# Loading early choices' results inside the experts' loop, and splitting the last choices' sums between two engines

## The chip, the cores and the metric

The kernel runs on one core of a Trainium2 chip. The core has five engines that run their own instruction streams: TensorE (PE, matrix products; PEld is its weight loads), VectorE (DVE), ScalarE (ACT), GpSimd (POOL) and SyncE (SP, used here as a queue that issues DMA transfers). An engine executes its stream in order, and waits on semaphores for the others. The metric is the device time of one execution in microseconds. Before the change the median of six runs is 678.52 us (674.44 to 679.24).

## The reference

Four transformer layers follow one another on 1024 tokens of width 256; each is a cross attention and a feed-forward block, both added to x. The change lies in the last block, a mixture of 64 experts of which each token uses 8:

```python
router_logits = x @ gate_w                                  # 1024 x 64
routing_weights, selected = jax.lax.top_k(router_logits, 8)
routing_weights = jax.nn.softmax(routing_weights, axis=-1)
gate = jax.lax.ragged_dot(hidden_sorted, gate_proj_w, group_sizes)
up   = jax.lax.ragged_dot(hidden_sorted, up_proj_w, group_sizes)
down = jax.lax.ragged_dot(jax.nn.silu(gate) * up, down_proj_w, group_sizes)
out  = jnp.sum(down[unsort].reshape(-1, 8, 256) * routing_weights[..., None], axis=1)
```

`hidden_sorted` holds every token's normed row 8 times, sorted by expert; `x` as used here is already normed, and `out` is added to the unnormed x.

## The kernel before

The 1024 tokens are 8 tiles of 128 (`NT = 8`). Everything up to the router is emitted by a planner (`Flow`): threads (`tile3`, `heads3`, `softmax3`, `scatter`, ...) yield operations with an engine and an assumed duration in us (`yield Op(DVE, 1.2, ...)`), and the planner decides from these durations and from due times in which order the operations stand on each engine. A changed duration can thus change the order of later operations.

*Routing* (`tile3`, one thread per tile). VectorE finds the 8 largest logits of each token (`sel`), TensorE counts each token's position within its expert (`pos`), and each chosen expert e gets the slot `e * CAP + pos` with `CAP = 192`. The kernel keeps `v = (NROWS - e * CAP) - pos` for the chosen experts and takes the 8 largest, so a token's choices 0 to 7 are sorted by expert, lowest first. Choice j can therefore only lie in experts up to 56 + j. A token whose position does not fit is marked in `over` (L1573), its rows are sent out of bounds, and it is done in a slow loop over all 64 experts behind a branch (L1757). `scatter` then puts a token's normed row, with the number of its result row, into `hs` in DRAM, with one indirect DMA for each tile and choice, generated by GpSimd (L1637): 64 puts.

*Experts* (`experts`). 32 pairs of experts (`n_pairs = 32`), p = 0 to 31. For each pair SP loads 384 rows (`load_rows`, six pairs ahead, L1739), TensorE turns them (L1800) and multiplies them with gate and up weights (L1849), ScalarE and VectorE make silu times up (L1855, L1857), TensorE multiplies with the down weights (L1867), VectorE and ScalarE copy the results out of PSUM (L1872), and GpSimd puts them with three indirect DMAs into `yd`, at each token's row for that choice (L1874). Weights come in groups of four experts into six buffers of tag `wt`. VectorE also makes one diagonal matrix per pair, of a tile's weights for one choice (L1888); `ON_PE = (4, 5, 6, 7)` names the choices that TensorE adds.

*Results.* `load_results(jp)` loads choices 2jp and 2jp + 1 of all tokens back from `yd` (2 MB) in two halves (jp = 3 in four quarters) on SP's queue, L1815. It waits for the puts of those pairs in which the choices can lie: jp = 0, 1, 2, 3 are issued at pairs 28, 29, 30, 31. The first three take `wt` buffers, the last takes `cx` and `ctxT`.

*Sums* (`sums`). Choices 0 to 3 are added to x by VectorE (`add_result`, L1825, a scalar_tensor_tensor with two inputs in SBUF): four of these 32 adds stand in pair 30, the rest after the loop. Choices 4 to 7 are summed in PSUM by TensorE with the diagonals (`sum_result`, L1830: 32 sums, 64 matmuls), choices 4 and 5 of all tiles first, then 6 and 7 tile by tile. VectorE adds the PSUM tile to x (`add_to_x`, L1708), and ScalarE's queue stores it (L1915). The order in `experts` and `sums` is written out by hand.

Of the kernel before, what the change touches and what calls it, by code (L numbers as in the profile page):

```python
# [25 lines left out]
ALU = mybir.AluOpType  # L26
AX = mybir.AxisListType

P = 128
B, S, D = 4, 256, 256  # L30
NTOK = B * S
NT = NTOK // P
# [14 lines left out]
E3, I3, K3 = 64, 96, 8  # L47
ORDERED = {mybir.EngineType.PE, mybir.EngineType.DVE, mybir.EngineType.Activation,
           mybir.EngineType.Pool}
GROUP, WEIGHTS, FIRST = 4, 6, 2  # L50
AHEAD = 6
ON_PE = (4, 5, 6, 7)
CAP = 192
RPP = 2 * CAP // P
NROWS = E3 * CAP
# [10 lines left out]
PE, DVE, ACT, POOL, SP = "PE", "DVE", "ACT", "POOL", "SP"  # L66
# [160 lines left out]
def model(ctx: ExitStack, tc: tile.TileContext, a: dict, out: bass.AP):  # L227
    nc = tc.nc
    PSUM = bass.MemoryType.PSUM

    const = ctx.enter_context(tc.tile_pool(name="const", bufs=1))
# [11 lines left out]
    def held(pool, shape, name, dtype=F32):  # L243
        return pool.tile(shape, dtype, tag=name, name=name)
# [4 lines left out]
    def x_t(t):  # L249
        return xb[t // 2][:, t % 2, :]  # L250

    ident = held(const, [P, P], "ident")
# [60 lines left out]
        out=tri, in_=tri, pattern=[[1, P]], compare_op=ALU.is_gt, fill=0.0, base=0,  # L313
# [9 lines left out]
    rwo = held(const, [P, NT, E3], "rwo")  # L323
    slots = held(const, [P, NT, K3], "slots", I32)
    over = held(const, [P, NT], "over")
    choice_w = held(const, [P, NT, K3], "choice_w")
    tick = held(const, [1, 1], "tick")

# [65 lines left out]
    def needs(ld, group, wanted, reason):  # L394

        for w in wanted:
            tc.add_manual_dep(
                ld.ins, w.name,
                mybir.DependencyInfo(mybir.DependencyClass.Sync, mybir.DependencyReason.DATA),
                reason=reason,  # L400
            )
        tc.declare_no_dep(ld.ins, group=group, keep=wanted + readers, reason=reason)
        tc.add_to_no_dep_group(group, ld.ins)
        readers.append(ld.ins)

    def layers(nk):
# [1110 lines left out]
        def tile3(t, q, lane, left):  # L1517
# [44 lines left out]
                    ps.ap, onesb if u < t else tri, sel[:, u, :], start=u == 0, stop=u == t  # L1562
                )
            pos, places = ps.ap, Buf()
            yield Op(DVE, 1.2, (ps, SEL[t]), (places,))
            nc.vector.scalar_tensor_tensor(ok, pos, float(CAP), sel[:, t, :], ALU.is_lt, ALU.mult)

            nc.vector.tensor_sub(v, first, pos)
            nc.vector.tensor_mul(v, v, ok)
            nc.vector.max(top[:, 8 : 8 + K3], v)  # L1570

            spilt = over[:, t : t + 1]
            nc.vector.tensor_scalar(spilt, top[:, 7 + K3 : 8 + K3], 0.0, None, ALU.is_equal)  # L1573
            nc.vector.tensor_scalar(rest[:, 0:1], spilt, float(NROWS), float(NROWS), ALU.mult, ALU.add)
            nc.vector.tensor_scalar(
                slots[:, t, :], top[:, 8 : 8 + K3], -1.0, rest[:, 0:1], ALU.mult, ALU.add
# [130 lines left out]
    def add_to_x(t, y):  # L1707
        nc.vector.tensor_add(x_t(t), y, x_t(t))  # L1708
# [3 lines left out]
    def moe_tile(shape, tag, bufs):  # L1712
        return moe.tile(shape, F32, tag=tag, name=tag, bufs=bufs)
# [86 lines left out]
                nc.tensor.transpose(tp[:, j, :], hb[:, j, dc * P : (dc + 1) * P], ident)  # L1800
        return hbT, tps

    def load_results(jp):

        n = 2 if jp == 3 else NT // 2
        for h in range(2):
            if jp < 3:
                g = moe_tile([P, GROUP * (4 * I3 + D)], "wt", WEIGHTS)[:, : NT // 2 * 2 * D]
            else:
                g = (cx.rearrange("p t d -> p (t d)"), ctxT.rearrange("p c r -> p (c r)"))[h]  # L1810
            gats[jp, h] = g = g.rearrange("p (t j d) -> p t j d", t=NT // 2, j=2)
            for t0 in range(0, NT // 2, n):
                at = (h * NT // 2 + t0) * P * K3
                source = yd[at : at + n * P * K3, :].rearrange("(t p j) d -> p t j d", p=P, j=K3)
                ld = nc.sync.dma_start(  # L1815
                    g[:, t0 : t0 + n].rearrange("p t j d -> p t (j d)"),
                    source[:, :, 2 * jp : 2 * jp + 2, :].rearrange("p t j d -> p t (j d)"),
                )
                needs(ld, "back", backs[: RPP * (n_pairs - 3 + jp)], "results of these choices alone")

    def result(t, j):
        return gats[j // 2, t // (NT // 2)][:, t % (NT // 2), j % 2, :]

    def add_result(t, j):
        nc.vector.scalar_tensor_tensor(  # L1825
            x_t(t), result(t, j), choice_w[:, t, j : j + 1], x_t(t), ALU.mult, ALU.add
        )

    def sum_result(y, t, i):
        nc.tensor.matmul(  # L1830
            y, diag[:, t, i, :], result(t, ON_PE[i]), start=i == 0, stop=i == len(ON_PE) - 1
        )

    def experts():
        for p in range(in_early, AHEAD):
            load_rows(p)
        load_weights(FIRST)
        load_weights(FIRST + 1)
        hbT, tps = rows_turned(0)
        nc.scalar.copy(hbT[:, 0], tps[0])  # L1840
        nc.vector.tensor_copy(hbT[:, 1], tps[1])
        for p in range(n_pairs):
            e = 2 * p
            gu, dn = weights[e // GROUP]
            pg, pu = ps_mm([I3, 2, RPP, P // 2], "ps_g3"), ps_mm([I3, 2, RPP, P // 2], "ps_u3")
            for k, ps in enumerate((pg, pu)):
                for i in range(2):
                    for dc in range(2):
                        nc.tensor.matmul(  # L1849
                            ps[:, i], gu[:, (e + i) % GROUP, 2 * k + dc, :],  # L1850
                            hbT[:, dc, :, i * (P // 2) : (i + 1) * (P // 2)],
                            start=dc == 0, stop=dc == 1,
                        )
            g = moe_tile([I3, 2, RPP, P // 2], "g4", 2)
            nc.scalar.activation(g, pg, AF.Silu)  # L1855
            act = moe_tile([I3, 2, RPP, P // 2], "act3", 2)
            nc.vector.tensor_mul(act, pu, g)  # L1857
            if p + 1 < n_pairs:
                hbT, tps = rows_turned(p + 1)
                nc.scalar.copy(hbT[:, 0], tps[0])  # L1860
                nc.vector.tensor_copy(hbT[:, 1], tps[1])
            yb = moe_tile([P, RPP, D], "yb", 3)
            for js in ((0, 1), (2,)):
                y = ps_acc([P, len(js), D], "ps_y")
                for k, j in enumerate(js):
                    for i in range(2):
                        nc.tensor.matmul(  # L1867
                            y[i * (P // 2) : (i + 1) * (P // 2), k], act[:, i, j, :],
                            dn[:, (e + i) % GROUP, :], start=True, stop=True,
                        )  # L1870
                for k, j in enumerate(js):
                    (nc.scalar.copy if j == 1 else nc.vector.tensor_copy)(yb[:, j, :], y[:, k, :])  # L1872
            for j in range(RPP):
                put = nc.gpsimd.indirect_dma_start(  # L1874
                    out=yd[:, :],
                    out_offset=bass.IndirectOffsetOnAxis(
                        ap=hbs[p][:, j, D : D + 1].bitcast(I32), axis=0
                    ),
                    in_=yb[:, j, :], in_offset=None, bounds_check=NPAIR - 1, oob_is_err=False,
                )  # L1880
                tc.declare_no_dep(put.ins, group="back", reason="distinct rows")
                tc.add_to_no_dep_group("back", put.ins)
                backs.append(put.ins)

            n = NT * len(ON_PE)
            for k in range(p * n // n_pairs, (p + 1) * n // n_pairs):
                t, i = k // len(ON_PE), k % len(ON_PE)
                nc.vector.tensor_scalar(  # L1888
                    diag[:, t, i, :], ident, choice_w[:, t, ON_PE[i] : ON_PE[i] + 1], None, ALU.mult
                )  # L1890
            if p + AHEAD < n_pairs:
                load_rows(p + AHEAD)
            k = FIRST + 2 + p if p < WEIGHTS - 2 else p // 2 + WEIGHTS if p % 2 else 0
            if k and k < E3 // GROUP:
                load_weights(k)
            if p >= n_pairs - 4:
                load_results(p - (n_pairs - 4))
            if p == n_pairs - 2:
                for t in range(NT // 2):
                    add_result(t, 0)  # L1900

    def sums():

        ys = [(ps_mm if t < 4 else ps_acc if t < 6 else ps_tp)([P, D], "ps_sum") for t in range(NT)]
        for i in range(len(ON_PE) - 2):
            for t in range(NT):
                sum_result(ys[t], t, i)
        for j in range(K3 - len(ON_PE)):
            for t in range(0 if j else NT // 2, NT):
                add_result(t, j)  # L1910
        for t in range(NT):
            for i in range(len(ON_PE) - 2, len(ON_PE)):
                sum_result(ys[t], t, i)
            add_to_x(t, ys[t])
            nc.scalar.dma_start(out[t // 2, t % 2 * P : (t % 2 + 1) * P, :], x_t(t))  # L1915

    with tc.manual_schedule(engines=ORDERED | {mybir.EngineType.SP}):
        experts()
# [85 lines left out]
```

## Time and profile before

| What | us |
|---|---|
| Median of 6 runs | 678.52 |
| The profiled execution's own time | 677.34 |
| Its span, first to last instruction | 675.6 |
| Routing's last put starts (L1637) | 480.27 |
| First expert matmul (L1849) | 483.54 |
| Period of the experts' loop | 4.99 |
| Last pair's down product starts (L1867) | 644.21 |
| Last add to x starts (L1708) | 671.86 |

| Engine | busy us | share |
|---|---|---|
| PE | 616.5 | 91% |
| DVE | 457.0 | 68% |
| POOL | 403.9 | 60% |
| ACT | 346.7 | 51% |

All times below are counted from the start of the span. The profile's chain follows the work back from the last instruction to whatever released each step. The timeline lists instructions in order of time, merged where they are alike; in brackets is the idle time before an instruction and what ended it. The row of an indirect DMA on POOL is the time that GpSimd takes to generate it; the transfer lands later. The releaser of a wait for several semaphores is the one that came last by the profile.

### The profile page before, as it was taken

How to read it: one execution, taken by the hardware profiler on the slowest of the kernel's cores; microseconds unless marked ns; L12 is line 12 of the kernel's file. 1: busy time of each engine (PE TensorE's matmuls, PEld its weight loads, DVE VectorE, ACT ScalarE, POOL GpSimd, SP SyncE). 2: the span in 40 equal slices, each digit the busy share in tenths (PEclk: the TensorE clock that was granted, in tenths of full speed). 3: DMA queues.
4: the chain of work that ended last, by engine and by line, in shares of the span. 5: the costliest groups of instructions: out<-in, count | busy, mean ns of one | idle time of the engine just before them, and what ended most of it. 6: DMA issues, size and time to landing. Idle time of an engine off the chain costs nothing. (4 is left out here: it accounts for less than half of the span.)

```text
span 675.6 us, 11485 instructions
## 1 busy us (share of the span) xinstructions
PE 616.5 (91%) x3820; PEld 473.7 (70%) x3820; DVE 457.0 (68%) x1161; ACT 346.7 (51%) x894; POOL 403.9 (60%) x516
## 2 busy tenths in 40 slices
PE   5999799999999999999998998995499999999937
PEld 4765465687878766888777786763378788787726
DVE  5787656767898689779789898897143444444482
ACT  1242268468898885457875876874122222222200
POOL 5999897111365484838148778767456555665550
PEclk9999899999999989999999999897599999999979
DMA  8999999710001031000031110222699867874395
GB/s 276 383 386 203 202 207 211 247 48 2 1 12 54 22 107 45 1 1 1 1 103 40 64 63 32 88 72 86 193 320 308 262 216 279 262 222 147 120 338 187
DMA packets 56036, 98.16 MB, mean 145 GB/s; under 512 B 7121, under 2 KB 37576, under 8 KB 55968
## 3 DMA queue, kind: packets, MB, share of 16 engines
q1 hardware_dynamic: 46048, 78.40, 40.4%
q0 software_dynamic: 7680, 16.84, 7.1%
q10 hardware_dynamic: 2240, 2.10, 0.9%
q8 instruction: 33, 0.54, 0.4%
q14 instruction: 35, 0.29, 0.1%
HBM read 58.42 MB, written 43.07 MB: 150 GB/s over the span
## 5 line engine op out<-in xcount | busy, mean ns | idle before, releaser
L1874 POOL DMA_INDIRECT yd<-yb,hb x84 | 85.9, 1023 | 57.7 <-DVE yb L1872 38.5
L1637 POOL DMA_INDIRECT hs<-hx,slots x64 | 66.2, 1034 | 25.7 <-issue 9.7
L1857 DVE TENSOR_TENSOR act<-ps_u,g 96x384 f32<-96x384 f32 x32 | 17.7, 554 | 73.6 <-ACT g L1855 63.6
L852 POOL TENSOR_TENSOR st<-st,mhalf 128x1 f32<-128x1 f32 x56 | 33.3, 598 | 53.4 <-DVE st L848 41.1
L1472 ACT ACTIVATE e<-ps_s,nm 128x128 f32<-128x128 f32 x128 | 46.1, 416 | 15.2 <-DVE nm L1466 15.1
L1439 POOL TENSOR_TENSOR q<-rt 64x512 f32<-64x512 f32 x32 | 43.7, 1365 | 7.5 <-DVE rt L1435 4.3
L1867 PE MATMUL ps_y<-wt,act 96*64 96x256 f32 x336 | 42.4, 388 | 2.0 <-DVE act L1857 0.7
L1849 PE MATMUL ps_g<-hbT,wt 128*96 128x192 f32 x224 | 43.1, 336 | 0.0
L1849 PEld LDWEIGHTS ps_g<-hbT,wt 128*96 128x96 f32 x224 | 34.1, 162 | 10.8 <-issue 10.8
L1849 PE MATMUL ps_u<-hbT,wt 128*96 128x192 f32 x224 | 41.0, 326 | 0.0
L1872 DVE COPY yb<-ps_y 128x256 f32<-128x256 f32 x64 | 27.2, 425 | 19.5 <-PE ps_y L1867 19.3
L1384 POOL TENSOR_TENSOR hh<-g,v 128x512 f32<-128x512 f32 x16 | 20.4, 1284 | 28.8 <-ACT g L1382 26.9
L1849 PEld LDWEIGHTS ps_u<-hbT,wt 128*96 128x96 f32 x224 | 36.4, 163 | 0.0
L1872 ACT COPY yb<-ps_y 128x256 f32<-128x256 f32 x32 | 11.9, 373 | 46.3 <-DVE yb L1872 32.3
L1460 PEld LDWEIGHTS ps_s<-keys,q 128*128 128x128 f32 x256 | 34.2, 195 | 1.2
L1855 ACT ACTIVATE g<-ps_g 96x384 f32<-96x384 f32 x32 | 15.6, 487 | 37.6 <-PE ps_g L1849 37.6
L1460 PE MATMUL ps_s<-keys,q 128*128 128x128 f32 x256 | 34.4, 278 | 0.0
L1860 ACT COPY hbT<-tp_hb 128x384 f32<-128x384 f32 x31 | 14.9, 479 | 36.4 <-PE tp_hb L1800 36.4
L1867 PEld LDWEIGHTS ps_y<-wt,act 96*64 96x64 f32 x336 | 21.6, 136 | 16.8 <-DVE act L1857 8.7
L855 DVE TENSOR_SCALAR h<-x,st 128x256 f32<-128x256 f32 x56 | 28.5, 516 | 6.6 <-POOL st L852 5.9
L1472 ACT ACTIVATION_READ_ACCUMULATOR e<-ps_s,nm 128x1 f32 x128 | 32.2, 255 | 0.0
L1105 ACT ACTIVATE e<-ps_s,nb 128x256 f32<-128x256 f32 x64 | 30.1, 490 | 3.9 <-DVE nb L1102 3.9
(337 smaller groups left out, 1731.7 us busy)
## 6 DMA issues: line engine op xcount, KB each, us to landing
hs<-blank_row SPq DMA_DIRECT2D x1, 12336.0 KB, 92.8
hb<-hs SPq DMA_DIRECT2D x28, 385.5 KB, 4.8
wt<-in_w_gu SPq DMA_DIRECT2D x14, 768.0 KB, 7.1
yd<-blank SPq DMA_DIRECT2D x1, 8192.0 KB, 29.5
wt<-yd SPq DMA_DIRECT2D x6, 1024.0 KB, 7.6
wt<-in_w_dn SPq DMA_DIRECT2D x14, 384.0 KB, 8.9
wo<-in_w_o SPq DMA_DIRECT2D x2, 1024.0 KB, 5.6
w<-in_w SPq DMA_DIRECT2D x2, 704.0 KB, 10.8
```

The costliest lines, as they stand in the source:

```text
L852: nc.gpsimd.tensor_tensor(s[:, 8:9], s[:, 7:8], mhalf, ALU.pow)
L855: nc.vector.tensor_scalar(h[:, k, :], x_t(t), ss[k][:, 6:7], ss[k][:, 8:9], ALU.subtract, ALU.mult)
L1105: nc.scalar.activation(e[:, mt, :], s[:, mt, :], AF.Exp, bias=nb[:, mt : mt + 1], accum_out=tot[:, 2 * j + mt : 2 * j + mt + 1],)
L1384: nc.gpsimd.tensor_mul(hh[:, cols], g.ap, v.ap)
L1439: nc.gpsimd.tensor_add(qv(q[i])[r, hps, :], t0[r], t1[r])
L1460: nc.tensor.matmul(s.ap[:, k, :], qv(q[hd % 2])[:, hd // 2, rows], keys3[:, hd % 2, b * S : b * S + nk * P], start=False, stop=k == n - 1,)
L1472: nc.scalar.activation(wide[:, k, :], s.ap[:, k, :], AF.Exp, bias=nm[:, k : k + 1], accum_out=tot[:, k : k + 1],)
L1637: put = nc.gpsimd.indirect_dma_start(out=hs[:, :], out_offset=bass.IndirectOffsetOnAxis(ap=slots[:, t, j : j + 1], axis=0), in_=rows[:, j, ...
L1849: nc.tensor.matmul(ps[:, i], gu[:, (e + i) % GROUP, 2 * k + dc, :], hbT[:, dc, :, i * (P // 2) : (i + 1) * (P // 2)], start=dc == 0, stop= ...
L1867: nc.tensor.matmul(y[i * (P // 2) : (i + 1) * (P // 2), k], act[:, i, j, :], dn[:, (e + i) % GROUP, :], start=True, stop=True,)
L1872: (nc.scalar.copy if j == 1 else nc.vector.tensor_copy)(yb[:, j, :], y[:, k, :])
L1874: put = nc.gpsimd.indirect_dma_start(out=yd[:, :], out_offset=bass.IndirectOffsetOnAxis(ap=hbs[p][:, j, D : D + 1].bitcast(I32), axis=0), ...
```

## The change

- A bound per choice, `BOUND = (48, 48, 58, 58, 64, 64, 64, 64)`: a token is marked in `over` also when one of its choices lies at or above the choice's bound. Instead of one comparison with zero there are a comparison of 8 values with a constant tile `bound` and a maximum over them. The planner's duration for this step goes from 1.2 to 1.4 us. The constant is written by eight memsets on GpSimd at the start.
- Choices 0 and 1 are now confined to pairs 0 to 23 and loaded at pair 23; choices 2 and 3 to pairs 0 to 28, loaded at pair 28; choices 4 and 5 are loaded at pair 30, 6 and 7 at pair 31, as before. Choices 4 and 5 go into the two buffers that choices 0 and 1 had.
- VectorE adds choices 0 and 1 in pairs 26 to 29 (four adds each), choice 2 in pairs 30 and 31, choice 3 after the loop.
- Choices 6 and 7 of the odd tiles are added by VectorE; TensorE sums choices 4 and 5 of all tiles, and 6 and 7 of the even ones. There are 24 diagonals instead of 32. TensorE does the odd tiles' sums first.

```diff
+BOUND = (48, 48, 58, 58, E3, E3, E3, E3)
@@ constants
+    bound = held(const, [P, K3], "bound")
+    for j in range(K3):
+        nc.gpsimd.memset(bound[:, j : j + 1], float(NROWS - BOUND[j] * CAP))
@@ tile3
-            yield Op(DVE, 1.2, (ps, SEL[t]), (places,))
+            yield Op(DVE, 1.4, (ps, SEL[t]), (places,))
...
-            nc.vector.tensor_scalar(spilt, top[:, 7 + K3 : 8 + K3], 0.0, None, ALU.is_equal)
+            nc.vector.tensor_tensor(rest[:, 1 : 1 + K3], top[:, 8 : 8 + K3], bound, ALU.is_le)
+            nc.vector.tensor_reduce(spilt, rest[:, 1 : 1 + K3], AX.X, ALU.max)
@@ load_results
-    def load_results(jp):
+    def load_results(jp, p):
...
-            if jp < 3:
+            if jp < 2:
                 g = moe_tile([P, GROUP * (4 * I3 + D)], "wt", WEIGHTS)[:, : NT // 2 * 2 * D]
+            elif jp == 2:
+                g = gats[0, h]
...
-                needs(ld, "back", backs[: RPP * (n_pairs - 3 + jp)], "results of these choices alone")
+                needs(ld, "back", backs[: RPP * (p + 1)], "results of these choices alone")
@@ ahead of experts
+    loaded = {}
+    for jp in range(K3 // 2):
+        last = max(min(BOUND[j] - 1, E3 - K3 + j) // 2 for j in (2 * jp, 2 * jp + 1))
+        loaded.setdefault(last, []).append(jp)
+    added = [(t, j) for j in range(ON_PE[0]) for t in range(NT)]
+    on_pe = [(t, j) for t in range(NT) for j in ON_PE if j in ON_PE[:2] or t % 2 == 0]
@@ experts
-            if p >= n_pairs - 4:
-                load_results(p - (n_pairs - 4))
-            if p == n_pairs - 2:
-                for t in range(NT // 2):
-                    add_result(t, 0)
+            for jp in loaded.get(p, ()):
+                load_results(jp, p)
+            for jp in (0, 1):
+                lead = p - min(q for q in loaded if jp in loaded[q]) - (3, 2)[jp]
+                if lead >= 0:
+                    for t, j in [k for k in added if k[1] // 2 == jp][4 * lead : 4 * (lead + 1)]:
+                        add_result(t, j)
@@ sums
+        at = min(q for q in loaded if 1 in loaded[q]) + 2
+        for t, j in added[2 * NT + 4 * (n_pairs - at) :]:
+            add_result(t, j)
...
+        for t in range(1, NT, 2):
+            for j in ON_PE[:2]:
+                sum_result(ys[t], t, j, ON_PE[0], ON_PE[1])
+        for t in range(0, NT, 2):
+            for j in ON_PE[:2]:
+                sum_result(ys[t], t, j, ON_PE[0], ON_PE[3])
+        for t in range(1, NT, 2):
+            add_to_x(t, ys[t])
         for t in range(NT):
+            for j in ON_PE[2:]:
+                if t % 2:
+                    add_result(t, j)
+                else:
+                    sum_result(ys[t], t, j, ON_PE[0], ON_PE[3])
+            if t % 2:
+                store(t)
+                add_to_x(t - 1, ys[t - 1])
+                store(t - 1)
```

More of the change, by code (lines that the diff above doesn't have):

```diff
@@ L1801, in rows_turned @@
         return hbT, tps
[L1803 removed]
+    def load_results(jp, p):
         n = 2 if jp == 3 else NT // 2
         for h in range(2):
[L1807 removed]
+            if jp < 2:
                 g = moe_tile([P, GROUP * (4 * I3 + D)], "wt", WEIGHTS)[:, : NT // 2 * 2 * D]
+                g = g.rearrange("p (t j d) -> p t j d", t=NT // 2, j=2)
+            elif jp == 2:
+                g = gats[0, h]
             else:
                 g = (cx.rearrange("p t d -> p (t d)"), ctxT.rearrange("p c r -> p (c r)"))[h]
[L1811 removed]
+                g = g.rearrange("p (t j d) -> p t j d", t=NT // 2, j=2)
+            gats[jp, h] = g
             for t0 in range(0, NT // 2, n):
@@ L1827, in add_result, with sum_result @@
         )
[L1829 to L1832, printed above, removed]
+    def sum_result(y, t, j, first, last):
+        nc.tensor.matmul(y, diag[:, t, j - ON_PE[0], :], result(t, j), start=j == first, stop=j == last)
+    loaded = {}
[4 more added lines that the diff above has]
+    on_pe = [(t, j) for t in range(NT) for j in ON_PE if j in ON_PE[:2] or t % 2 == 0]
     def experts():
@@ L1883, in experts @@
                 backs.append(put.ins)
-            n = NT * len(ON_PE)
-            for k in range(p * n // n_pairs, (p + 1) * n // n_pairs):
-                t, i = k // len(ON_PE), k % len(ON_PE)
+            n = len(on_pe)
+            for t, j in on_pe[p * n // n_pairs : (p + 1) * n // n_pairs]:
                 nc.vector.tensor_scalar(
-                    diag[:, t, i, :], ident, choice_w[:, t, ON_PE[i] : ON_PE[i] + 1], None, ALU.mult
+                    diag[:, t, j - ON_PE[0], :], ident, choice_w[:, t, j : j + 1], None, ALU.mult
                 )
@@ L1895, in experts, with store @@
                 load_weights(k)
-            if p >= n_pairs - 4:
-                load_results(p - (n_pairs - 4))
-            if p == n_pairs - 2:
-                for t in range(NT // 2):
-                    add_result(t, 0)
-    def sums():
-        ys = [(ps_mm if t < 4 else ps_acc if t < 6 else ps_tp)([P, D], "ps_sum") for t in range(NT)]
[L1905 to L1910, printed above, removed]
-        for t in range(NT):
[L1912 to L1915, printed above, removed]
+            for jp in loaded.get(p, ()):
[5 more added lines that the diff above has]
+                        add_result(t, j)
+    def sums():
+        def store(t):
+            nc.scalar.dma_start(out[t // 2, t % 2 * P : (t % 2 + 1) * P, :], x_t(t))
+        at = min(q for q in loaded if 1 in loaded[q]) + 2
+        for t, j in added[2 * NT + 4 * (n_pairs - at) :]:
+            add_result(t, j)
+        ys = [(ps_mm if t < 4 else ps_acc if t < 6 else ps_tp)([P, D], "ps_sum") for t in range(NT)]
+        for t in range(1, NT, 2):
[6 more added lines that the diff above has]
+            add_to_x(t, ys[t])
+        for t in range(NT):
+            for j in ON_PE[2:]:
[7 more added lines that the diff above has]
+                store(t - 1)
     with tc.manual_schedule(engines=ORDERED | {mybir.EngineType.SP}):
```

## The prediction

> **What bounds the kernel now.** I first read the chain that ended last, over the end of the span. Columns: start, length, what.
>
> ```profile
> 642.33 1.21 POOL yd L1874
> 643.85 5.35 DMA yd<-yb,hb
> 649.34 6.93 DMA wt<-yd
> 656.32 15.52 PE ps_sum L1830 x64
> 671.86 0.42 DVE x L1708
> ```
>
> Until about 642 us the chain sits in the experts' loop, which repeats every 4.99 us. After it come four things that cannot overlap: the last put of pair 30 landing, the load of choices 4 and 5 that waited for it, 15.52 us of TensorE adding choices 4 to 7, and one VectorE add; the stores then run out to 675.6. So what the change is worth is read from 642 us on. There I read the timeline, and a narrow one of SP's queue for the two issue times it merges:
>
> ```profile
> 641.42 1.67 DVE L1825 SCALAR_TENSOR_TENSOR x<-wt,choice_w,x 128x256 f32<-128x256 f32 x4
> 642.33 1.21 POOL L1874 DMA_INDIRECT yd<-yb,hb  x1 [0.30 <-issue]
> 643.60 0.55 DVE L1857 TENSOR_TENSOR act<-ps_u,g 96x384 f32<-96x384 f32 x1 [0.51 <-issue]
> 644.33 0.91 SPq L1815 DMA_DIRECT2D wt<-yd  x2
> 646.30 6.42 DVE L1825 SCALAR_TENSOR_TENSOR x<-wt,choice_w,x 128x256 f32<-128x256 f32 x16
> 648.73 4.84 POOL L1874 DMA_INDIRECT yd<-yb,hb  x1 [0.30 <-DVE x L1825]
> 649.34 0.91 SPq L1815 DMA_DIRECT2D wt<-yd  x2
> 653.65 4.84 DVE L1825 SCALAR_TENSOR_TENSOR x<-wt,choice_w,x 128x256 f32<-128x256 f32 x12 [0.93 <-DMA wt<-yd]
> 658.54 0.87 SPq L1815 DMA_DIRECT2D cx<-yd  x2
> 664.76 3.62 PE L1830 MATMUL ps_sum<-cx,diag 128*128 128x256 f32 x16
> ```
>
> The reader should see a convoy. Choices 0 and 1 are loaded at 636.15, after pair 28. While their 2 MB move, the last put of pair 29 (638.62 to 639.59) lands only just before 644.33, where it lets choices 2 and 3 go. While those move, pair 30's last put (to 644.82) lands at 649.25, and choices 4 and 5 go at 649.34. Without a load in front, pair 28's last put ended at 634.60 and was landed by 636.15. Also to be seen: the last put of all takes 4.84 us beside a run of 16 VectorE adds, and ends 0.85 us after that run does.
>
> TensorE idles from 645.7 on and starts its sums cold. Columns: busy time per engine, granted clock, DMA share, GB/s.
>
> ```profile
> 656.00:658.00 2.00, 1.68 (x4) 1.42 (x5) 2.00 (x6) 0.00 (x0) 0.00 (x0) 0.50 0.97 361
> 660.00:662.00 2.00, 2.00 (x11) 1.76 (x10) 0.00 (x0) 0.00 (x0) 0.00 (x0) 1.00 0.93 258
> ```
>
> Last, the routing stage, whose test is edited, by its timeline:
>
> ```profile
> 468.33 0.15 DVE L1573 TENSOR_SCALAR over<-top 128x1 f32<-128x1 f32 x1
> 468.71 0.38 DVE L1575 TENSOR_SCALAR slots<-top,w 128x8 int32<-128x8 f32 x1
> 469.85 0.97 POOL L1637 DMA_INDIRECT hs<-hx,slots  x1 [0.69 <-ACT w L1587]
> 480.27 0.97 POOL L1637 DMA_INDIRECT hs<-hx,slots  x1 [0.23 <-issue]
> 482.92 0.20 ACT L1790 ACTIVATE silu<-mhalf 128x1 f32<-128x1 f32 x1 [2.63 <-POOLq L1757]
> ```
>
> The last tile's slots start nine puts on POOL, and the experts' loop begins only behind them.
>
> **The change, part by part.** *Loads.* Choices 0 and 1 go after pair 23; choices 2 and 3 take their old place after pair 28; 4 and 5 stay at pair 30, 6 and 7 at 31. So nothing moves ahead of pair 30's last put except choices 2 and 3, issued at 636.15 and, like their predecessors (first half read at 641.42), done before 644. That put should land 1.5 us (pair 28's) to 3.0 us (pair 22's: 604.67 to 607.71) after its end, at 646.4 to 647.8. I take 646.8, nearer to pair 28, the later row with less other traffic: 2.4 us earlier than 649.25.
>
> The load of choices 4 and 5 reaches TensorE after 6.93 us now, behind the tail of the earlier load; the shortest landing of such a load is 5.2. I take 5.8, since pair 31's puts share the engines: landed at 652.6, where it was 656.3. It also waits for the buffer that choices 0 and 1 leave; those adds end in pair 29, some 8 us before.
>
> *TensorE after the loop.* The first 16 sums take 656.32 to 664.76 = 8.4 us, their cold start included; after 6.9 us idle it stays cold (the granted clock fell to 0.75 in 648 to 650 and 0.50 after), so they end at 661.0. Then 8 sums instead of 16: four tiles at 0.865 us (the spacing of the adds at the end of the timeline), 664.5 instead of 671.8.
>
> *VectorE after the loop.* Odd tiles now get choices 6 and 7 here: two adds of 0.40 (6.42 / 16) and one of 0.42 for the neighbour make 1.22 us per two tiles, more than TensorE's 0.865, so VectorE ends it: first sum added by 662.3, and 3 x 1.22 more: 666.0. Before, the last add ended at 672.28. **Tail: -6.3 us**, the stores (3.3 us) unchanged.
>
> The cover is the load of choices 6 and 7, late next. VectorE's run after the last pair shrinks from 16 adds to 12 (4.8 us, to 651.1); the last put, if held to the end of that run, ends at 652.0 and lands when the second half of choices 4 and 5 is in, about 655.3 (1 MB at the 390 GB/s of the windows is 2.7 us after the first). Its four loads then land 4.2, 4.2, 6.0 and 6.7 us after issues 0.5 apart, the last at 663.5; VectorE needs that one at about 664.8. So 1.3 us of cover, then microsecond for microsecond. With everything as late as before (issue 658.54, last landing 666.7, then 1.22) the tail still gains 4.4 us; with 1.5 and 5.2 us for the landings above it gains 7.3.
>
> The row of 4.84 us is a put held by adds with both inputs in SBUF. The Trainium skill, page "SBUF — State Buffer", section "Who interferes with whom", has the rule: a VectorE instruction with two SBUF inputs contends with a GpSimd instruction that reads SBUF, and the second to issue blocks. That row agrees, the put at 647.32 (1.10 us inside the same run) does not. By the rule the 16 adds moved into pairs 26 to 29 hold each pair's second put to the end of its run, 0.4 us (642.33 would end at 643.94, not 643.54); by the row of 1.21 us, 0.24 us. Either way the sum stays, since POOL idles 1.46 us per pair waiting for VectorE.
>
> *VectorE in the loop.* The adds of pairs 26 to 29 and 31 fall where pair 30's four stood: 641.42 to 643.09, with 0.51 us left before L1857 at 643.60, exactly one period after 638.61. So nothing, if the data is there. Queued behind a late load would be that L1857, then TensorE. Choices 0 and 1 go after pair 23's puts and one row load, near 612.5 (row loads go at 607.71 and 612.1 here), and land by 618.7 to 621; their first use is at 641.42 - 4 x 4.99 = 621.5. Bounds 0 to +2 us; I take 0. On SP the row loads of pairs 30 and 31 now stand behind these two loads, with five periods of lead. Eight fewer diagonals (0.28 each) save 2.2 us of an engine busy 2.15 of 5 us: nothing.
>
> *Routing.* Per tile a 128x8 compare and reduce replace one instruction of 0.15; the nearest rows (128x8 at 0.16 to 0.23, a reduce at 0.17 to 0.22) add about 0.2. On the last tile that moves the slots from 469.1 to 469.3, before the put at 469.85. Eight tiles: 0 to 2 us, VectorE being about 88% busy here. The planner was also given 1.4 for 1.2, and from the first such test on the order on all four engines differs, though not the work. Rows for what an order is worth here: POOL's waits of 3.91 us (447.00) and 1.18 us (459.63) before a put; one may come or go: -3 to +4. I take +0.7 for all. Eight more POOL memsets (starts 0.03 to 0.04 us apart) fit in its 0.49 us wait near 3.1 us.
>
> **Sum.** 677.3 for the profiled execution (span 675.6 and 1.7 around it) - 6.3 + 0.7 = 671.7. That execution lies 1.2 below the median of 678.5, so 672.9 for a median.
>
> **Rivals.** *The last transfer becomes the bound:* the last put lands as late as now. For it: 4.84 us under 16 adds, while 12 remain. Against it: less traffic ahead. -4.4 + 0.7: 674.8.
>
> *The new order in the routing stage costs a wait or two:* +4 to +8 instead of +0.7: 676 to 680. For it: waits of 3.91 us exist. Against: the work is the same and the last two tiles keep nearly their order.
>
> *Puts locked out in the loop (slower):* if every pair from 26 on holds a put as at 648.73, by 3.9 us, POOL falls 3.9 - 1.46 = 2.4 us behind in each of six pairs, 14.6 us, and everything after the loop moves with it: 678.5 + 14.6 - 5.6 = 687.5. It passes slower-by-0.5% once a hold exceeds about 3 us (six times (hold - 1.46) over 5.6 + 3.4). Against it: pair 30's run of four held its put 0.24 us, and a run ends 1.67 us after it starts.
>
> *The bound sends tokens to the leftover loop:* routed by the reference on its inputs, the highest experts of choices 0 to 3 are 39, 42, 48 and 55, under 48, 48, 58 and 58, so none goes there. 0.01; 64 turns, each with a weight load of the 7 us kind, some 450 us.
>
> **How the numbers follow.** The median of six runs spans 0.7%, so 0.5% (3.4 us: 675.1, 681.9) is about what can be told from no change. Forecast 0.58 (670 to 675.1); a better order in routing, 667 to 670, 0.05; last transfer 0.13, split about the line; routing waits 0.15, nearly all within; locked puts 0.06, an order in routing dearer than 9 us 0.02, leftover 0.01. Faster 0.69, same 0.21, slower 0.10. The range reaches from a tail of 7.3 with a good order, 668, to the routing rival's end, 680.
>
> **What would show it.** Right: a load of results near 612 us; the load for choices 4 and 5 about 2.5 us earlier against the last pair; a period still 4.99 us in pairs 26 to 29; 48 instead of 64 matmuls of ps_sum; the loads of choices 6 and 7 about 3 us earlier. Wrong: a put over 2 us in pairs 26 to 30, L1857's counterpart waiting on wt<-yd, or a first expert matmul later than 483.5 by more than 2 us.

## The result and the profile after

The changed kernel takes 675.75 us (median of 36 runs, 672.11 to 677.68) where the kernel before takes 678.54 (73 runs beside them): a ratio of 0.996, with a 95% interval of 0.995 to 0.997. So it is faster, by 2.8 us; 5.6 had been predicted. The profiled execution took 673.94 us, with a span of 672.1, 3.5 us less than before.

The span of both profiles can be cut at three instructions that both kernels have: the first tile's `slots` in the routing, the first expert matmul, and the last pair's down product.

| Stretch of the span, us | before | after | difference |
|---|---|---|---|
| start to the first slots | 350.75 | 350.56 | -0.2 |
| first slots to first expert matmul (routing) | 132.79 | 135.12 | +2.3 |
| first expert matmul to last down product (loop) | 160.67 | 160.06 | -0.6 |
| last down product to the end (tail) | 31.39 | 26.36 | -5.0 |

In this pair of profiles, each of one execution, the tail gave 5.0 of the 6.3 us forecast, and routing took 2.3 back where 0.7 had been put down.

First the loop, in the timeline of the changed kernel, in the lines that answer to those of pair 30 before:

```profile
613.68 1.01 SPq L1827 DMA_DIRECT2D wt<-yd  x2
622.90 1.66 DVE L1837 SCALAR_TENSOR_TENSOR x<-wt,choice_w,x 128x256 f32<-128x256 f32 x4
623.91 1.10 POOL L1893 DMA_INDIRECT yd<-yb,hb  x1 [0.30 <-issue]
625.18 0.55 DVE L1876 TENSOR_TENSOR act<-ps_u,g 96x384 f32<-96x384 f32 x1 [0.62 <-issue]
643.17 1.67 DVE L1837 SCALAR_TENSOR_TENSOR x<-wt,choice_w,x 128x256 f32<-128x256 f32 x4 [0.23 <-DMA wt<-yd]
645.13 0.55 DVE L1876 TENSOR_TENSOR act<-ps_u,g 96x384 f32<-96x384 f32 x1 [0.30 <-issue]
```

Choices 0 and 1 are loaded at 613.68. Four adds end 0.62 us before the product that the chain needs (L1876), which recurs at 630.17, 635.16 and 640.15: the period is still 4.99 us. A put beside such adds takes 1.10 us and not 0.97 (0.97 to 1.11 in pairs 26 to 30). Pair 30's adds wait 0.23 us for their load and still leave 0.30.

Then the tail, the same timeline (SP's two rows as its own queue shows them):

```profile
647.84 4.83 DVE L1837 SCALAR_TENSOR_TENSOR x<-wt,choice_w,x 128x256 f32<-128x256 f32 x12
650.26 3.26 POOL L1893 DMA_INDIRECT yd<-yb,hb  x1 [0.30 <-DVE x L1837]
656.74 0.87 SPq L1827 DMA_DIRECT2D cx<-yd  x2
657.66 1.81 SPq L1827 DMA_DIRECT2D ctxT<-yd  x2
662.22 7.26 ACTq L1925 DMA_DIRECT2D out<-x  x8
665.43 1.13 PE L1842 MATMUL ps_sum<-ctxT,diag 128*128 128x256 f32 x4 [1.39 <-DMA ctxT<-yd]
666.76 1.90 PE L1842 MATMUL ps_sum<-ctxT,diag 128*128 128x256 f32 x4 [0.20 <-DMA ctxT<-yd]
668.69 0.42 DVE L1716 TENSOR_TENSOR x<-ps_sum,x 128x256 f32<-128x256 f32 x1 [0.76 <-PE ps_sum L1842]
```

and the end of the chain:

```profile
657.66 1.29 SPq L1827
659.00 7.72 DMA ctxT<-yd
666.76 1.91 PE ps_sum L1842 x4
```

The last put (650.26) is still held until 0.85 us after VectorE's run ends, but the run is four adds shorter, and the loads that wait for the put go at 656.74 (11.00 us after the last down product, before 14.33). The chain no longer runs through 15.52 us of sums: it runs through the last quarter of the last load, and then through four matmuls that take 1.90 us; the last four of the profile before took 1.03 us. The windows of the changed kernel show the clock at the start and at the end of the sums (columns: length; PE, PEld, DVE, ACT, POOL busy; granted clock, DMA share, GB/s):

```profile
656.00:657.00 1.00, 1.00 (x5) 0.80 (x4) 0.15 (x1) 0.00 (x0) 0.00 (x0) 0.64 0.03 8
667.00:668.00 1.00, 1.00 (x3) 0.76 (x3) 0.90 (x3) 0.00 (x0) 0.00 (x0) 0.50 0.50 171
```

TensorE had its full clock back from 656.73 on, waited 1.39 us for data, and lost it again at 666.97: 0.50 for the last four matmuls. The trace's record of the clock helps to read this. In all 18 profiles of this case any two changes of the granted clock lie a whole multiple of 3.41 us apart (649.90, 656.73 and 666.97 here). In the 3.41 us that ended with the loss TensorE idled for 1.39 + 0.20 us; 1.07 us of idling in such a stretch (`after_again`, below) and 0.94 us (`t_actq`) left the clock at 1.00.

### The profile page after: what moved, and what is told of

The parts are those of the page before. It is cut to its first block, busy times and chain, and to the rows that moved or that the text cites. A ratio compares the mean times of both kernels' runs of the same rounds, so it can differ in the third digit from the quotient of the medians.

```text
span 672.1 us, 11459 instructions
## 1 busy us (share of the span) xinstructions
PE 610.9 (91%) x3804; PEld 468.3 (70%) x3804; DVE 461.2 (69%) x1169; ACT 346.5 (52%) x894; POOL 403.0 (60%) x524
## 5 line engine op out<-in xcount | busy, mean ns | idle before, releaser
L1876 DVE TENSOR_TENSOR act<-ps_u,g 96x384 f32<-96x384 f32 x32 | 17.7, 554 | 68.6 <-ACT g L1874 42.4
L1891 ACT COPY yb<-ps_y 128x256 f32<-128x256 f32 x32 | 11.9, 373 | 46.3 <-DVE yb L1891 32.1
L1431 PE MATMUL ps_q<-qc,wq 96*128 96x256 f32 x128 | 30.8, 382 | 2.4 <-DVE rt L1441 1.3
```

The source lines that it names most:

```text
L1431: nc.tensor.matmul(ps.ap[:, k, :], w[:, hp * P : (hp + 1) * P], qc.ap, start=True, stop=True)
```

## Experiments: the whole change again, on other chips

Each group of runs was measured beside the kernel before on one chip, and the chips differ: the kernel before takes 678.5 us on the first, 688.0 on chip 14, 693.3 on chip 7, 688.3 on chip 13 and 688.7 on chip 4. Only ratios of one group are compared. The changed kernel was measured again in three groups, and the kernel before was profiled once more:

> The changed kernel itself, unaltered, as the yardstick on the chip of the next three. From the first result (ratio 0.996): 2.8 us below before. From the last pair's down product to the end 26.4 us in its first profile, where before had 31.4; if the 5.0 us are a property of the kernel and not of one execution, 25.8 to 26.8 again.

> The changed kernel once more, beside the other three of this call, so that each of them can be read against it on one chip. The tail, from the last pair's down product to the end of the span, was 26.36 and 25.34 us in the two executions seen so far: expected 25 to 26.5. If the routing stage is as long as on the first chip (133 to 135 us), the gain over the kernel before should again be near 2.8 us; if it is long (141 to 149 us), the gain should be 5 to 8 us, which would tie the size of the gain to the chip's routing stage. The rival, that the larger gain of the second measurement was chance, expects 2.8 us in either case.

> The changed kernel once more, beside the two of this call. Tail 24.7 to 26.4 us, as in the three executions seen. Gain over the kernel before: 5 to 8 us if the routing edit costs nothing here, 2.5 to 4 if it costs about 2 us.

> The kernel before, unchanged, for a profile of its routing stage on whatever chip this call gets. Theory, that the length of that stage belongs to the chip: on a chip where the kernel before takes 688 to 693 us its stage is 141 to 146 us long, with stalls of VectorE of 2 to 4 us that no wait of the first profile has. Rival, that the edit lengthens the stage: the stage is 133 us as in the first profile, and the longer time lies elsewhere. The time itself is within 0.3% of the kernel before.

| Run (chip) | ratio, 95% interval | routing | tail |
|---|---|---|---|
| before (first) | 1 | 132.79 | 31.39 |
| after (first) | 0.996, 0.995 to 0.997 | 135.12 | 26.36 |
| after_again (7) | 0.9875, 0.9834 to 0.9916 | 143.45 | 25.34 |
| after_third (13) | 0.9907, 0.9874 to 0.994 | 142.49 | 24.70 |
| after_fourth (4) | 0.9931, 0.9896 to 0.9966 | 145.07 | 26.04 |
| before_again (4) | 0.9999, 0.9973 to 1.0024 | 141.38 | 32.66 |

By these ratios the gain is 8.7, 6.4 and 4.8 us on the three other chips: 2.8 us is the smallest of four. The routing stage of the *unchanged* kernel takes 141.38 us on chip 4 and 132.79 on the first, so most of the extra length belongs to the chip (or to what else goes on there) and not to the edit. The larger gain goes with the long stage only loosely: chip 4 has it too, and its interval touches the first one's.

What ended the tail on chip 4 is what had been forecast for the first. VectorE's timeline of `after_fourth`:

```profile
675.34 0.42 DVE L1716 TENSOR_TENSOR x<-ps_sum,x 128x256 f32<-128x256 f32 x1 [2.51 <-PE ps_sum L1842]
675.68 0.99 DVE L1837 SCALAR_TENSOR_TENSOR x<-cx,choice_w,x 128x256 f32<-128x256 f32 x2
676.59 0.42 DVE L1716 TENSOR_TENSOR x<-ps_sum,x 128x256 f32<-128x256 f32 x1
676.92 1.00 DVE L1837 SCALAR_TENSOR_TENSOR x<-ctxT,choice_w,x 128x256 f32<-128x256 f32 x2
677.84 0.42 DVE L1716 TENSOR_TENSOR x<-ps_sum,x 128x256 f32<-128x256 f32 x1
678.17 0.99 DVE L1837 SCALAR_TENSOR_TENSOR x<-ctxT,choice_w,x 128x256 f32<-128x256 f32 x2
679.08 0.42 DVE L1716 TENSOR_TENSOR x<-ps_sum,x 128x256 f32<-128x256 f32 x1
```

No row waits for a load; the sums come every 1.25 us (1.22 predicted). What made the difference to the first profile is the start of the sums. The windows of `after_fourth` from 1.5 us after their start:

```profile
666.00:668.00 2.00, 2.00 (x6) 1.63 (x5) 0.42 (x1) 0.00 (x0) 0.00 (x0) 0.50 0.36 135
668.00:670.00 2.00, 2.00 (x6) 1.56 (x5) 0.43 (x1) 0.00 (x0) 0.00 (x0) 0.50 0.62 141
```

The clock stayed at 0.50 for over 5 us, and the first 16 sums took 9.93 us, against 8.70 in the first profile. In that time the last loads landed, so their lateness did not show. The two costs cover one another; the tail is 26.0 us by the one and 26.4 by the other. With the sums at 9.06 us and the loads just in time it is 24.70 (`after_third`).

The second profile of the kernel before shows what the early loads are worth. Four rows of `before_again`; SP's row holds the issues of choices 2 and 3 and of choices 4 and 5 together:

```profile
653.75 0.97 POOL L1874 DMA_INDIRECT yd<-yb,hb  x1 [0.30 <-issue]
654.34 1.52 PE L1867 MATMUL ps_y<-wt,act 96*64 96x256 f32 x12 [0.70 <-issue]
654.51 2.83 SPq L1815 DMA_DIRECT2D wt<-yd  x4
665.48 9.98 PE L1830 MATMUL ps_sum<-wt,diag 128*128 128x256 f32 x32 [9.62 <-DMA wt<-yd]
```

Here the load of choices 4 and 5 goes at 656.35, 2.0 us after the last down product (2.1 and 2.2 in `r_only` and `r_only2` below, which also keep the old loads), as early as in the changed kernel. In the first profile it went 5.1 us after it, because pair 30's last put landed late. That lateness is not in every execution: the load of choices 2 and 3 was issued 0.49 us before this put's end in the first profile, 0.21 us before it here. Yet in all four the sums start late, 11.1 to 12.1 us after the last down product, because 2 MB of choices 2 and 3 are still in front; in the kernels with the early loads they start after 7.4 to 8.0 us. So the early loads gain by taking 2 MB out of the line, whether or not the put is late.

## Experiments: the tail, one part at a time

**Early loads alone, split alone.** `t_nosplit` keeps the early loads and lets TensorE sum all of choices 4 to 7; `l_split_alone` keeps the places of the loads and the test of the kernel before, and splits the sums.

```diff
 t_nosplit
-    on_pe = [(t, j) for t in range(NT) for j in ON_PE if j in ON_PE[:2] or t % 2 == 0]
+    on_pe = [(t, j) for t in range(NT) for j in ON_PE]
 l_split_alone
-    loaded = {23: [0], 28: [1], 30: [2], 31: [3]}
+    loaded = {28: [0], 29: [1], 30: [2], 31: [3]}
```

> The changed kernel without the split: TensorE sums choices 4 to 7 of all tiles (32 sums), VectorE adds only the sums. Theory (the landing of the last quarter ends the tail, not the engines): TensorE reaches choices 6 and 7 at about 662 and needs 16 sums of 0.43 us, so it ends near 669.1 and stays at full clock; the time is 0 to 1 us above the changed kernel. Rival (the split gains what the eight sums cost, as predicted): 3 to 3.5 us above the changed kernel, about that of before.

> The split of the last choices alone, with the old routing test: all loads where they were before (after pairs 28, 29, 30, 31), VectorE's adds of choices 0 to 3 as before, but choices 6 and 7 of the odd tiles on VectorE. Theory (the landing of the last loads sets the end, and they go no earlier here than before, 14.3 us behind the last pair's down product; the changed kernel ends 15.4 us behind that issue): 29 to 30 us from the down product to the end, 1.5 to 2.5 us below before. Rival (eight sums fewer are worth their TensorE time): 27.5 to 28 us, 3.5 us below before.

Measured: 0.9971 (0.9938 to 1.0004), tail 28.15 us; and 0.9976 (0.9944 to 1.0008), tail 30.03 us. The four profiles with the old tail (the two of before, and `r_only`, `r_only2` below) have 31.39, 32.66, 32.19 and 32.09: 32.1 on average. The seven with the whole new tail (the four of after, and `r_cost12`, `r_cost12b`, `r_oldtest` below) have 24.70 to 26.36: 25.8 on average. So in the tail the early loads alone give 3.9 us, the split alone 2.1, and both 6.3: the parts nearly add up, with one execution for each part. The medians are less clear: 2.0 and 1.7 us of gain, and both intervals hold 1. Beside kernels with both parts on the same chip, `t_nosplit` is 2.0 to 4.1 us slower (`r_cost12`, `r_oldtest`, `t_freeput`), nearer to its rival than to its theory, and `l_split_alone` 5.6 to 7.0 us slower (`t_free12`, `after_again`). What each part leaves undone is seen in the timelines of `t_nosplit`,

```profile
672.31 3.62 PE L1842 MATMUL ps_sum<-cx,diag 128*128 128x256 f32 x16
675.76 3.62 PE L1842 MATMUL ps_sum<-ctxT,diag 128*128 128x256 f32 x16
679.42 0.42 DVE L1716 TENSOR_TENSOR x<-ps_sum,x 128x256 f32<-128x256 f32 x1 [0.44 <-PE ps_sum L1842]
```

where the loads are early but TensorE has 16 sums left without a gap, and of `l_split_alone`,

```profile
666.49 4.84 POOL L1884 DMA_INDIRECT yd<-yb,hb  x1 [0.30 <-DVE x L1831]
673.73 9.74 PE L1836 MATMUL ps_sum<-wt,diag 128*128 128x256 f32 x32 [10.24 <-DMA wt<-yd]
676.28 0.87 SPq L1821 DMA_DIRECT2D cx<-yd  x2
```

where half of those sums are gone, but the put is held for 4.84 us and TensorE starts 10.24 us after its last work (6.43 us in `after_fourth`).

**The last put set free.** Choice 3's adds that stood ahead of the sums go behind the odd tiles' first sums. `t_free12` has the planner's 1.2 besides.

```diff
-        for t, j in added[2 * NT + 4 * (n_pairs - at) :]:
-            add_result(t, j)
+        late = added[2 * NT + 4 * (n_pairs - at) :]
...
-        for t in range(1, NT, 2):
+        for t, n in zip(range(1, NT, 2), (2, 1, 1, len(late))):
             add_to_x(t, ys[t])
+            for u, j in late[:n]:
+                add_result(u, j)
+            del late[:n]
```

> The changed kernel with VectorE's eight adds of choice 3 moved from right behind the loop to behind the first add of a PSUM sum, where VectorE waits anyway; four adds stay beside the last puts. Theory (the last put is held by the run of adds and that delays the last loads): the put takes about 1 us instead of 3.26, the loads of choices 6 and 7 go 1 to 2 us earlier than at 656.7, and the time falls 1 to 2 us below the changed kernel. Rival (the put's landing waits for the transfer of choices 4 and 5 in any case): the put takes 1 us, the loads still go at 656.2 to 656.8, and the time is that of the changed kernel within 0.5 us.

> VectorE's adds of choice 3 are moved behind the first three sums of the odd tiles, so that the last put has no VectorE run beside it; all work is done. It was 24.85 us of tail once. Theory, that the landing of the last loads sets the end: the put's 2.3 us of hold fall away, but its landing still follows the transfer of choices 4 and 5, so the loads go 0.5 us earlier and the kernel is 0.5 to 1.5 us faster than the changed kernel of this call. Rival, that the put's hold is what keeps the loads: 2.3 us faster. If VectorE's adds become the bound instead: 0 to 1 us slower.

> The changed kernel with the eight adds of choice 3 moved behind the first sum's add, as in the run before with that edit, and the planner's duration back at 1.2. That run's last put took 0.97 us, the last loads went 10.5 us behind the last pair's down product (11.0 in the others), and the end came 24.9 us behind it. Theory (the freed put is worth 1 to 1.5 us): 24.5 to 25.3 us from the down product to the end, 1 to 1.5 us below the changed kernel on this chip, and more if the order in routing costs something: up to 3 us below it. Rival (that run's tail was chance): 25.9 to 26.4 us and the changed kernel's time.

The rows of `t_freeput2`, POOL and SP:

```profile
660.77 0.97 POOL L1893 DMA_INDIRECT yd<-yb,hb  x1 [0.31 <-issue]
666.71 0.87 SPq L1827 DMA_DIRECT2D cx<-yd  x2
667.64 0.97 SPq L1827 DMA_DIRECT2D ctxT<-yd  x2
```

The put takes 0.97 us instead of 3.26, so the adds beside it did hold it. But the loads go 10.46 us after the last down product instead of 11.00: the put, over by 661.74, lets them go only at 666.71. The windows show 400 and 404 GB/s from 664.08 to 666.08 and 119 in the next microsecond, so that is when the 2 MB of choices 4 and 5 are through. The put landed late behind a load here, and that hides most of the hold. The times: 0.9914 (0.9883 to 0.9945) on chip 13 beside 0.9907 for `after_third`; `t_free12` 0.9897 (0.9859 to 0.9934) on chip 7 beside 0.9875 for `after_again`; `t_freeput` 0.9905 (0.987 to 0.994) on chip 14, its tail 24.85 us, 26.05 and 26.00 in the others. No gain over the changed kernel can be seen.

**TensorE kept busy.** `t_warm` adds seven products with zeros ahead of the last two pairs of sums.

```diff
         for t in range(NT):
+            if t in (4, 6):
+                for _ in range(4 if t == 4 else 3):
+                    nc.tensor.matmul(ys[t], blank[:, :P], result(0, 4), start=False, stop=False)
```

> Seven products with a zero matrix are added on TensorE ahead of the last two pairs of sums, four before tile 4's and three before tile 6's, so that TensorE does not idle while the last loads land; they add zero to the sums. Theory, that the last four sums ran at a granted clock of 0.50 because TensorE had idled: they take 0.9 to 1.2 us instead of 1.90, and the tail loses 0.7 to 1.0 us. Rival, that the landing alone sets the end and the slow sums are something else (their data arriving): the four sums still take 1.7 to 1.9 us and the time is within 0.3 us of the changed kernel.

TensorE's timeline:

```profile
671.82 1.24 PE L1943 MATMUL ps_sum<-wt,blank 128*128 128x256 f32 x5
672.90 1.03 PE L1842 MATMUL ps_sum<-ctxT,diag 128*128 128x256 f32 x4
673.77 1.46 PE L1943 MATMUL ps_sum<-wt,blank 128*128 128x256 f32 x6
675.06 1.03 PE L1842 MATMUL ps_sum<-ctxT,diag 128*128 128x256 f32 x4
```

The last four matmuls take 1.03 us, as the theory of the clock said, but this does not test it: they take 1.03 to 1.13 us without the added products too, in all profiles but the first of the changed kernel. In this execution the first sums took 10.02 us, TensorE had no gap to fill, and the added products (1.89 and 1.46 us in all) stand ahead of the last sums; the tail is 27.36 us. The time is 0.9966 (0.9937 to 0.9995) beside 0.9907, so the products probably cost more than they save. That the slow last sums of the first profile come from idling rests on the clock record shown with the result.

**The last loads on another queue.** In `t_actq` ScalarE's queue issues the two loads into `ctxT`.

```diff
-                ld = nc.sync.dma_start(
+                ld = (nc.scalar if jp == 3 and h else nc.sync).dma_start(
```

> The last two of the four loads of choices 6 and 7 (into ctxT) are issued from ScalarE's queue instead of SyncE's, so that they do not stand behind the first two. Theory, that the end is set by the issue on one queue (four issues took 2.7 us, the third alone 1.29): the last issue comes 1.0 to 1.5 us earlier, the last landing 0.8 to 1.5 us earlier, and the tail loses as much. Rival, that the landings share a full transfer path with the stores and with one another: the issues come earlier, the last landing does not, and the time is within 0.4 us of the changed kernel.

The loads were issued 0.17 us after the first into `cx` instead of 0.93 (`after_third`), and the pair took 1.89 us there too. The adds of the odd tiles then waited for `cx`, whose second quarter was there only some 7.9 us after its issue (5.2 in the profile after):

```profile
670.12 1.00 DVE L1837 SCALAR_TENSOR_TENSOR x<-cx,choice_w,x 128x256 f32<-128x256 f32 x2 [1.24 <-DMA cx<-yd]
673.65 1.00 DVE L1837 SCALAR_TENSOR_TENSOR x<-cx,choice_w,x 128x256 f32<-128x256 f32 x2 [0.46 <-DMA cx<-yd]
673.67 1.13 PE L1842 MATMUL ps_sum<-cx,diag 128*128 128x256 f32 x4 [0.94 <-DMA cx<-yd]
```

Time 0.996 (0.9926 to 0.9994), tail 26.94 us; the first sums took 10.13 us here and 9.06 in `after_third`. The earlier issue did not bring the end forward, so issue on one queue is not the limit. From 668.7 to 673.7 the 16 DMA engines were busy 86 to 105% of the time by the windows, which fits the rival, that the loads share one full path; the time, though, is about 3.6 us longer than that of `after_third`, with intervals that just overlap, where the rival expected no change. That their order on one queue is of use would explain the late `cx`, but no run shows it apart.

## Experiments: the routing stage

`r_only` and `r_only2` are the kernel before with the routing edit alone; `r_cost12` and `r_cost12b` the changed kernel with the old order of instructions; `r_oldtest` the changed kernel with the old order and the old test, so it leaves out the bound.

```diff
 r_cost12, r_cost12b, r_oldtest (r_only: the other way round)
-            yield Op(DVE, 1.4, (ps, SEL[t]), (places,))
+            yield Op(DVE, 1.2, (ps, SEL[t]), (places,))
 r_oldtest
-            nc.vector.tensor_tensor(rest[:, 1 : 1 + K3], top[:, 8 : 8 + K3], bound, ALU.is_le)
-            nc.vector.tensor_reduce(spilt, rest[:, 1 : 1 + K3], AX.X, ALU.max)
+            nc.vector.tensor_scalar(spilt, top[:, 7 + K3 : 8 + K3], 0.0, None, ALU.is_equal)
```

> The kernel before with the routing part of the change alone: the bound constants, the two-instruction test and the planner's 1.4; loads, loop and sums as before. Theory (the new routing costs about 2 us, as the first pair of profiles has it: first expert matmul at 485.68 instead of 483.54): 1.5 to 2.5 us above before. Rival (routing costs 0 to 0.7 us as predicted, and the 2.1 us are scatter of single executions): 0 to 0.7 us above before. The stretch after the loop as before, 31.4 us, under both.

> The kernel before with the routing edit alone (the new test, the constant, the planner's 1.4), once more; loads, adds and sums as before. If the edit costs what the two first profiles differ by in that stage: +1.5 to +2.3 us. If it costs its instructions only: 0 to +1. If the first of these measurements (1.1 us faster, between 2.0 faster and none) holds: -2 to 0.

> The changed kernel with the planner's duration of the routing test set back to 1.2, so that the order on all engines is the one of before, while the two-instruction test stays. In the changed kernel the first expert matmul starts at 485.68 instead of 483.54, and the last pair's down product at 645.74 instead of 644.21. Theory (the order did it): first expert matmul at 483.8 to 484.3, the time about 1.5 us below the changed kernel, 4 to 4.5 us below before. Rival (the added VectorE instructions did it): first expert matmul still at 485.4 to 485.9, the time that of the changed kernel, 2.8 us below before.

> The changed kernel with the planner's duration of the routing test put back from 1.4 to 1.2, so that the order of the instructions is that of the kernel before while the new test stays, once more. If the new order costs: 1.5 to 2.5 us faster than after_fourth. If it does not: within 1 us of it. If the new order gains: slower by 1 to 3 us.

> The changed kernel with the old routing test of one instruction, its old duration in the planner, and no bound constants; the early loads stay, so that a token beyond the bound would not be caught (the reference's inputs have none). Both theories: first expert matmul at 483.5, and the gain after the loop alone, about 5.0 us below before. If the order did it, this is within 0.5 us of the run with the duration set back; if the instructions did it, it is 1.5 to 2 us below that run.

| Run (chip) | order, test | ratio, 95% interval | routing |
|---|---|---|---|
| r_only (7) | new, new | 0.9971, 0.9941 to 1.0001 | 143.55 |
| r_only2 (4) | new, new | 1.0001, 0.9977 to 1.0024 | 144.70 |
| r_cost12 (14) | old, new | 0.992, 0.9891 to 0.9949 | 146.97 |
| r_oldtest (14) | old, old | 0.9912, 0.9887 to 0.9937 | 143.00 |
| r_cost12b (4) | old, new | 0.9929, 0.99 to 0.9959 | 141.61 |

The profiles contradict one another on what the order costs. On chip 4 the old order has 141.4 and 141.6 us and the new 144.7 and 145.1, which looks like the first pair of profiles (132.79 and 135.12). But the old order has 147.0 and 143.0 on chip 14, where the kernels with the new order, `t_freeput` and `t_nosplit`, have 140.9 and 143.0; and 149.2 (`l_split_alone`) and 143.2 (`t_free12`) on chip 7, where the new has 143.5 and 143.6. What the order does is seen inside the stage: in all eleven profiles with the new order the third slots come 39.7 to 39.8 us after the first and the fourth 68.1 to 68.5, in all seven with the old one 42.1 to 45.9 and 61.7 to 65.7. By the eighth slots this is gone: 119.9 to 130.4 against 118.0 to 133.8. One execution is a sample here: the single times of the kernel before spread over 8 us on chip 13 and on chip 4. The medians see nothing: the edit alone is 0.29% faster and 0.01% slower (both intervals hold 1, and `r_only` fits neither its theory nor its rival), and the old order gives 0.9929 on chip 4 where the new gives 0.9931. On the first chip, where the intervals are tight, no part was tried alone. That the edit costs 2.3 us there is what one pair of profiles shows; whether its order does, stays open.

## Why the prediction was right or wrong

The direction was right, the range (668 to 680) holds 675.75, and the size was twice what was measured on that chip. Two terms of the sum failed, by the one pair of profiles from that chip: the tail of -6.3 gave -5.0, since the cover of the last load was taken too large, and the +0.7 of routing was +2.3. The loop and the start took 0.8 us less, so the spans differ by 3.5 us and the medians by 2.8. The first failure is seen in the trace; why routing took longer there stays open.

- **The load of choices 4 and 5** goes 2.11 us after the last down product (at 647.86) instead of 5.13: 3.0 us earlier, 2.4 predicted. It reaches TensorE after 5.76 us (5.8). The sums thus start 4.2 us earlier against the last down product, where 3.7 had been forecast. The convoy was read rightly for that execution, but the late put in it was partly chance: without it the load goes at 2.0 to 2.2 us in the old order too and then takes 9.1 to 9.8 us to reach TensorE. The load of choices 2 and 3 was not "done before 644" as assumed: its predecessor's second half landed at 644.90, its own at 646.52. Pair 30's put landed 1.7 us after its end even so.
- **The first 16 sums:** 8.70 us in the row, 8.60 in the same row of the profile before (8.4 to the next sums). Right for that execution by luck; 8.74 to 10.13 in the others, by how long the clock stayed at 0.50.
- **The last put and the loads behind it:** held to 0.85 us past VectorE's run as assumed; loads issued at 656.74, where the prediction's 655.3 moved by the 1.5 us by which the last down product came later makes 656.8. Right.
- **The cover of the last load, "1.3 us of cover, then microsecond for microsecond", failed.** The third issue alone took 1.29 us instead of some 0.5, the landings were 4.4, 5.2, 7.7 and 7.7 us (4.2, 4.2, 6.0 and 6.7 assumed, from a profile in which the stores began at 666.27; here they start at 662.22, which may be why, but no run shows it). The last quarter landed at 666.72 where 665.0 had been expected, in the same shift: 1.7 us late, 0.4 beyond the cover. And past the cover it is not microsecond for microsecond: TensorE, left idle, lost its clock, and 1.91 us of sums take the place of VectorE's adds, so the last add ends 2.39 us after the landing and not 1.22. Tail -5.0 instead of -6.3: -4.7 to the end of the last add, and 0.35 us less for the stores behind it. This is the rival in which the last transfer becomes the bound (674.8), for another reason than the put.
- Over all profiled executions the tail loses 32.1 - 25.8 = 6.3 us. On average the size was right. That owes something to chance too: the first pair joins the shortest of the four old tails (31.39) and the longest of the seven new ones (26.36), and the sums were assumed to take 8.4 us where the four old profiles have 8.60 to 9.98.
- **Routing, "I take +0.7 for all", was mis-sized on the first chip:** +2.3 in its profiles. The instructions cost what was said (0.17 and 0.16 for 0.15); the warning sign that had been named, a first expert matmul later than 483.5 by more than 2 us, came (485.68). Elsewhere the medians of the edit alone give -2.0 and +0.1 us, so whether the edit costs 2.3 us on the first chip or that execution was long by chance is not known.
- **The loop, 0:** right. Period 4.99, no wait of L1876 for a load, adds of pairs 26 to 30 ended 0.30 to 0.8 us before it. Locked puts did not come: at most 1.11 us beside a run of four adds. The Trainium skill, page "SBUF — State Buffer", section "Who interferes with whom", has a VectorE instruction with two SBUF inputs contend with a GpSimd instruction that reads SBUF, and the one that issues second wait until the other's instruction is over. That is one add of some 0.4 us, where the prediction took the whole run. The trace shows a wait for a whole run of adds only of the last put (3.26 us, and 9.59 us beside 28 adds in `before_again`), not of those in the loop.

## What to carry to other kernels

Work at the end that waits for a transfer can be shortened on both sides: the bytes that stand in line in front of the transfer, and the work that is left behind it. Here the two gave 3.9 and 2.1 us of the tail's 6.3. A put can land late behind a large load that is already under way, so freeing the last put alone bought 0.5 us of its 2.3; whether it does can differ from one execution to the next, so read more than one profile before counting on it. And where a stage's time differs by several microseconds from run to run, one pair of profiles says nothing of an edit that is worth one or two.

## What the runs showed of the hardware beside that

- The first 350 us are the same on all chips (350.06 to 351.94), and the routing stage behind them takes 132.8 and 135.1 us on the first and 140.6 to 149.2 on the four others (the kernel before itself: 132.79 and 141.38). Part of it is a wait that the first chip's two profiles lack and thirteen of the sixteen others have, 2.4 us long or longer; two without any such wait of VectorE, `r_oldtest` and `t_free12`, still take 143 us. VectorE's row in `before_again`; the releaser, "remote", is nothing that the profile explains, and the cause stays open:

```profile
446.61 0.43 DVE L876 TENSOR_TENSOR x<-ps_y,x 128x256 f32<-128x256 f32 x1 [3.25 <-remote]
```

- The pair of issues into `ctxT` takes 0.97 to 1.12 us in most kernels with the old tail or with the put set free, and 1.62 to 2.20 in those with the changed one (3.09 in `r_only2`). Why was not settled.
- TensorE at 0.50 after idling gets its full clock back after 3.1 us of sums in one execution and after 5.6 in another, which alone moves these 16 sums by 1.2 us (8.70 against 9.93). The steps of 3.41 us in the clock's record account for it in all 18 profiles: where the sums begin at most 0.48 us into such a step, the clock is back at its end (2.93 to 3.21 us later); where they begin 0.80 us into it or later, at the end of the next one (3.45 to 6.03 us later). Where in a step they begin differs from one execution to the next.
